# Layer 0's destination rows by one-hot matmul behind an earlier branch, and layer 1's node rows made inside layer 0's MLP loop

## The chip, the cores and the metric

One core of a Trainium2 chip runs the whole kernel in one launch. A core has five engines that each take their own instructions in order: PE (TensorE, matmuls; its weight loads, PEld, are shown apart), DVE (VectorE), ACT (ScalarE), POOL (GpSimd, which here issues the gathers) and SP (SyncE, which issues the plain DMAs). They meet through semaphores. The metric is the device time of one execution in microseconds (us); lower is better. The number for a kernel is the median of several runs.

## The reference

A graph network of four layers, each a graph step (`gnn`) and a per-node network (`ffn`), each on a layernorm of x and added to it. x has 3125 rows (nodes) of 256; there are 53125 edges sorted by destination, 50000 of them random and one loop per node. The change touches the two steps of layer 0 and the beginning of layer 1's graph step:

```python
def _L0_gnn_ref(...):
    xt = jnp.matmul(x, weight).reshape(-1, heads, out_ch)          # 4 heads of 64
    row, col = (edge_index[0], edge_index[1])
    alpha_l = jnp.einsum('ehd,hd->eh', xt[row], attn_l)
    alpha_r = jnp.einsum('ehd,hd->eh', xt[col], attn_r)
    alpha = jax.nn.softmax(jax.nn.leaky_relu(alpha_l + alpha_r, 0.01), axis=1)
    tmp = jnp.einsum('nh,nhd->nd', alpha[:n], xt[col[:n]])         # the first 3125 edges only
    out = jnp.broadcast_to(tmp[:, None, :], (n, heads, out_ch))

def _L0_ffn_ref(...):
    weights = (jnp.einsum('bsd,do->bso', x, wr) + br)[..., 0]      # one score per row
    _, idx = jax.lax.top_k(weights, k)                             # the better half, less one
    h = jax.nn.gelu(jnp.einsum('bkd,dh->bkh', sel, w1) + b1)       # 256 -> 1024
    y = jnp.einsum('bkh,hd->bkd', h, w2) + b2                      # 1024 -> 256
    y = y * w_sel[..., None]
    return processed + x                                           # rows not chosen: x

def _L1_gnn_ref(...):
    q = (x @ Wq + bq).reshape(n, H, C)
    k = (x @ Wk + bk).reshape(n, H, C)
    v = (x @ Wv + bv).reshape(n, H, C)
    e = (edge_attr @ We).reshape(-1, H, C)
    ...                                                            # attention over the edges
    out = out + x @ Ws + bs
```

Only the first 3125 edges count in layer 0's graph step, since `alpha` is cut to n rows.

## The kernel before

x stays on the chip as 25 tiles of 128 rows (`self.x`, 3200 rows with padding). The edges are 416 tiles of 128; 8 edge tiles (`EL`) make a window. As the edges are sorted by destination, the destinations of a window lie within 128 successive rows that begin at `W0[g]`, a constant. A flag worked out on the device (`prepare_flags`) says whether the input is so ordered; `sorted_edges()` reads it, and a branch takes the path that uses windows (`l1_gnn_sorted`, `after_l1_gnn_sorted`) or a general one.

The order of the instructions on each engine is fixed when the kernel is built, by a scheduler that goes by the dependences and by the buffers of the pools: a tile that is asked for again under the same name gets one of `bufs` buffers, and waits until its last reader is done.

What runs, in order:

- `l0_gnn` (L1407). Layernorm of x, and per tile of 128 rows a product with the weight and the two attention vectors; 264 columns go to the DRAM table `xt_d`, and the four columns of `alpha_l` once more to `al_d`. SP issues these 50 writes. `prepare_loads` loads what the flag and the indices need. Then five chunks of five edge tiles: for each tile POOL gathers `z` (4 values a row, by source) and `g` (264 values, by destination), both at L258; DVE and ACT do the softmax over the four heads and the weighted sum (L1435 to L1450), and the last line adds it to x.
- `l0_ffn` (L1452). Zero fills of tables that later layers need; layernorm of x, added to x (L234), transposed to `xT`; the row score `wa` for all rows; its copy by column, `wt` (L1487). Then the MLP over seven groups (`GROUPS`: six of four tiles, one of one): for each of eight hidden blocks a product of 128x512 into `ph` (two buffers) and a gelu on ACT (L1497), then for each tile eight matmuls and a bias matmul into `po`, copied by ACT to `yo` (L1504). Beside it DVE counts for each row how many rows have a better score (L1513 to L1517), sums this to `rank` (L1521), and makes `cw` (L1523): the score where the row is among the chosen, else 0. `prepare_flags` follows. The last loop (L1526) does x += yo * cw per tile.
- the branch.
- `l1_gnn_sorted` (L501). Four weights and four biases are loaded; layernorm of x, transposed to `xT`; `project` makes 512 columns per tile with a bias matmul of three bf16 rows (`ones3`), in three `pkv` buffers: first all 25 tiles of k and v, copied by ACT (L537) and written to `kv_d`; then all 25 tiles of q and the skip term, q split into three bf16 parts by ACT and DVE (`split`, L441 to L445) and written to `q_d`, the skip term added to x (L544). Then the edge loop: edge attributes `ea` times `We`, gathers of k and v by source, and q of the destination by a one-hot product (`window`, L453 and L456, gives the one-hot `sT`).

`split` writes an f32 tile as three bf16 tiles whose sum is the tile: two operations on ACT, two on DVE. `window(load, g)` loads the window's local destinations, broadcast to 128 partitions (256 KB), and compares them with the partition's number.

Of the kernel before, what the change touches and what calls it, by code (L numbers as in the profile page):

```python
# [8 lines left out]
F32 = mybir.dt.float32  # L9
BF = mybir.dt.bfloat16  # L10
I32 = mybir.dt.int32
AF = mybir.ActivationFunctionType
ALU = mybir.AluOpType
AX = mybir.AxisListType
PSUM = bass.MemoryType.PSUM
DRAM = bass.MemoryType.DRAM

P = 128
D = 256
N = 3125  # L20
NT = 25
NP = NT * P
# [4 lines left out]
EL = 8  # L27
# [4 lines left out]
GROUPS = [(g, min(4, NT - g)) for g in range(0, NT, 4)]  # L32
# [3 lines left out]
W0 = [min(max(round(N * (g + 0.5) * EL * P / E) - P // 2, 0), NP - P) for g in range(NW)]  # L36
# [10 lines left out]
class Net:  # L47
# [445 lines left out]
    def accumulate(self, work, table, acc, g):  # L493
# [4 lines left out]
        nc.scalar.copy(o, acc)  # L498
        nc.gpsimd.dma_start(table[W0[g]:W0[g] + P, :], o, accum_op=ALU.add)

    def l1_gnn_sorted(self, wp):  # L501
        nc, tc = self.nc, self.tc
        scale = 1.0 / 32 ** 0.5
        wkv = wp.tile([P, 2, 2, D], F32, name="wkv")
        for j, n in enumerate("kv"):
            nc.sync.dma_start(wkv[:, :, j, :],
                              self.ins[f"L1_gnn_W{n}"].rearrange("(k p) n -> p k n", p=P))
        wqs = wp.tile([P, 2, 2, D], F32, name="wqs")
        for j, n in enumerate("qs"):
            nc.sync.dma_start(wqs[:, :, j, :],  # L510
                              self.ins[f"L1_gnn_W{n}"].rearrange("(k p) n -> p k n", p=P))
        bkv = self.bias3(wp, "L1_gnn_bk", "L1_gnn_bv")
        bqs = self.bias3(wp, "L1_gnn_bq", "L1_gnn_bs")
        we = self.rows(wp, "L1_gnn_We")
        with ExitStack() as ctx:
            dram = ctx.enter_context(tc.tile_pool(name="d1", bufs=1, space=DRAM))
            kv_d = dram.tile([NP, 2 * D], F32, name="kv_d")
            q_d = dram.tile([NP, 3, D], BF, name="q_d")
            acc_d = self.acc1_d
            with ExitStack() as ctx1:  # L520
                big = ctx1.enter_context(tc.tile_pool(name="big", bufs=1))
                work = ctx1.enter_context(tc.tile_pool(name="work", bufs=3))
                psum = ctx1.enter_context(tc.tile_pool(name="psum", bufs=2, space=PSUM))
                xT = big.tile([P, 2, NP], F32, name="xT")
                self.layernorm(work, psum, xT=xT)

                def project(t, w, b):
                    p = psum.tile([P, 2, D], F32, name="pkv", bufs=3)
                    self.mm(p.rearrange("p j n -> p (j n)"),
                            [(xT[:, k, t * P:(t + 1) * P], w[:, k].rearrange("p j n -> p (j n)"))  # L530
                             for k in range(2)] + [(self.ones3, b)])
                    return p

                for t in range(NT):
                    p = project(t, wkv, bkv)
                    kv = work.tile([P, 2, D], F32, name="kv", bufs=6)
                    nc.scalar.copy(kv, p)  # L537
                    nc.sync.dma_start(kv_d[t * P:(t + 1) * P, :], kv.rearrange("p j n -> p (j n)"))
                for t in range(NT):
                    p = project(t, wqs, bqs)  # L540
                    q = work.tile([P, 3, D], BF, name="q")
                    self.split(work, q, p[:, 0, :], D, "q")
                    nc.sync.dma_start(q_d[t * P:(t + 1) * P, :, :], q)
                    nc.vector.tensor_add(self.x[:, t, :], self.x[:, t, :], p[:, 1, :])  # L544
            big = ctx.enter_context(tc.tile_pool(name="big", bufs=1))
            load = ctx.enter_context(tc.tile_pool(name="load", bufs=2))
            work = ctx.enter_context(tc.tile_pool(name="work", bufs=3))
            psum = ctx.enter_context(tc.tile_pool(name="psum", bufs=2, space=PSUM))
# [7 lines left out]
            for c in range(ET // 2 + LAG):  # L556
                if c < ET // 2:
                    t = 2 * c
                    if t % EL == 0:
                        g = t // EL  # L560
                        ea = load.tile([P, 2, EL * P], F32, name="ea")
                        nc.sync.dma_start(ea, self.ins["edge_attr_256"][:, :, t * P:(t + EL) * P])
                        sT = self.window(load, g)
                        qw = load.tile([P, 3, D], BF, name="qw")
                        nc.sync.dma_start(qw, q_d[W0[g]:W0[g] + P, :, :])
                    kv = work.tile([P, 2, 2 * D + 8], F32, name="kv", bufs=LAG + 5)
# [3 lines left out]
                    for j in range(2):  # L570
                        self.gather(kv[:, j, :2 * D], kv_d, self.idx["src"][:, t + j:t + j + 1])
                        e = slice((t + j) % EL * P, ((t + j) % EL + 1) * P)
# [20 lines left out]
                b = c - LAG  # L593
                if b >= 0:
                    kv = kvs.pop(b)
                    t = 2 * b
# [810 lines left out]
    def l0_gnn(self, wp):  # L1407
        nc, tc = self.nc, self.tc
        w = self.with_attention(wp, "L0_gnn_weight", 4, ("L0_gnn_attn_l", "L0_gnn_attn_r"))
        with ExitStack() as ctx:  # L1410
            dram = ctx.enter_context(tc.tile_pool(name="d0", bufs=1, space=DRAM))
            big = ctx.enter_context(tc.tile_pool(name="big", bufs=1))
            work = ctx.enter_context(tc.tile_pool(name="work", bufs=3))
            psum = ctx.enter_context(tc.tile_pool(name="psum", bufs=2, space=PSUM))
            xt_d = dram.tile([NP, D + 8], F32, name="xt_d")
            al_d = dram.tile([NP, 4], F32, name="al_d")
            xT = big.tile([P, 2, NP], F32, name="xT")
            self.layernorm(work, psum, xT=xT)
            for t in range(NT):
                pt = psum.tile([P, D + 8], F32, name="pt")  # L1420
                self.mm(pt, [(xT[:, k, t * P:(t + 1) * P], w[:, k, :]) for k in range(2)])
                row = work.tile([P, D + 8], F32, name="row", bufs=6)
                nc.scalar.copy(row, pt)
                nc.sync.dma_start(xt_d[t * P:(t + 1) * P, :], row)
                nc.sync.dma_start(al_d[t * P:(t + 1) * P, :], row[:, D:D + 4])
            self.prepare_loads()

            C = 5
            for t0 in range(0, NT, C):
                z = work.tile([P, C, 4], F32, name="z")  # L1430
                g = work.tile([P, C, D + 8], F32, name="g")
                for j in range(C):
                    self.gather(z[:, j, :], al_d, self.idx["src"][:, t0 + j:t0 + j + 1])
                    self.gather(g[:, j, :], xt_d, self.idx["dst"][:, t0 + j:t0 + j + 1])
                nc.vector.tensor_add(z, z, g[:, :, D + 4:])  # L1435
                nc.vector.scalar_tensor_tensor(z, z, 0.01, z, op0=ALU.mult, op1=ALU.max)
                mx = work.tile([P, C], F32, name="mx")
                mb = mx.unsqueeze(2).to_broadcast([P, C, 4])
                nc.vector.tensor_reduce(mx, z, axis=AX.X, op=ALU.max)
                nc.vector.tensor_sub(z, z, mb)  # L1440
                nc.scalar.activation(z, z, AF.Exp)
                nc.vector.tensor_reduce(mx, z, axis=AX.X, op=ALU.add)
                nc.vector.reciprocal(mx, mx)
                nc.vector.tensor_mul(z, z, mb)
                gv = g[:, :, :D].rearrange("p t (h d) -> p t h d", h=4)
                nc.vector.tensor_mul(gv, gv, z.unsqueeze(3).to_broadcast([P, C, 4, 64]))
                nc.vector.tensor_add(gv[:, :, :2], gv[:, :, :2], gv[:, :, 2:])
                nc.vector.tensor_add(gv[:, :, 0, :], gv[:, :, 0, :], gv[:, :, 1, :])
                xv = self.x[:, t0:t0 + C, :].rearrange("p t (h d) -> p t h d", h=4)
                nc.vector.tensor_add(xv, xv, gv[:, :, :1, :].to_broadcast([P, C, 4, 64]))  # L1450

    def l0_ffn(self, wp):  # L1452

        nc, tc = self.nc, self.tc
        keep = int(0.5 * N) - 1
# [6 lines left out]
        with ExitStack() as ctx:  # L1462
# [58 lines left out]
            nc.vector.tensor_reduce(rank, cnt, axis=AX.X, op=ALU.add)  # L1521
            cw = big.tile([P, NT], F32, name="cw")
            nc.vector.scalar_tensor_tensor(cw, rank, float(keep), wt, op0=ALU.is_lt, op1=ALU.mult)  # L1523
            self.prepare_flags()
            for t in range(NT):
                nc.vector.scalar_tensor_tensor(self.x[:, t, :], yo[:, t, :], cw[:, t:t + 1],  # L1526
                                               self.x[:, t, :], op0=ALU.mult, op1=ALU.add)


    def l1_gnn(self, wp):  # L1530
# [684 lines left out]
@with_exitstack  # L2215
def tile_gnn_ffn(ctx: ExitStack, tc: tile.TileContext, ins, out):
    net = Net(ctx, tc, ins, out)

    def run(*layers):
        for layer in layers:  # L2220
            with tc.tile_pool(name="w", bufs=1) as wp:
                layer(wp)

    run(net.l0_gnn, net.l0_ffn)

    with tc.If(net.sorted_edges()) as cmp:
        run(net.l1_gnn_sorted, net.after_l1_gnn_sorted)
    with cmp.Else():
        run(net.l1_gnn, net.l1_ffn, net.l2_gnn, net.l2_ffn, net.l3_gnn, net.l3_ffn)


# [72 lines left out]
```

## Time and profile before

| what | us |
|---|---|
| median of 5 runs (lowest, highest) | 3863.33 (3857.88, 3866.10) |
| profiled execution | 3859.73 |
| its span in the profile | 3857.9 |
| first gather of layer 0 starts, last ends | 68.74, 136.38 |
| x complete after layer 0's edges | 150.9 |
| first MLP matmul of layer 0 | 179.66 |
| `cw` is made | 278.4 |
| last combine of layer 0 (L1526) | 363.4 |
| first matmul after the branch | 375.69 |
| last projection matmul of layer 1 ends | 495.4 |
| first add of the edge loop (L576) starts | 510.61 |

Times of single instructions are counted from the span's start. PE is busy 85% of the span, DVE 58%, POOL 43%, ACT 25%, and the mean granted clock of PE is 0.917. All that the change touches lies in the first 510 us; the rest is layer 1's edges and its network, and layers 2 and 3.

In the rows below, a group is named by line, engine, operation, output <- inputs, shape, type and count; behind the bar stand its busy time in us and the mean ns of one, then the idle time of its engine before it and what ended that. In a table by stage each engine has its busy time and, in brackets, the number of instructions.

### The profile page before, as it was taken

How to read it: one execution, taken by the hardware profiler on the slowest of the kernel's cores; microseconds unless marked ns; L12 is line 12 of the kernel's file. 1: busy time of each engine (PE TensorE's matmuls, PEld its weight loads, DVE VectorE, ACT ScalarE, POOL GpSimd, SP SyncE). 2: the span in 40 equal slices, each digit the busy share in tenths (PEclk: the TensorE clock that was granted, in tenths of full speed). 3: DMA queues.
4: the chain of work that ended last, by engine and by line, in shares of the span. 5: the costliest groups of instructions: out<-in, count | busy, mean ns of one | idle time of the engine just before them, and what ended most of it. 6: DMA issues, size and time to landing. Idle time of an engine off the chain costs nothing. (4 is left out here: it accounts for less than half of the span.)

```text
span 3857.9 us, 46616 instructions
## 1 busy us (share of the span) xinstructions
PE 3283.2 (85%) x15463; PEld 2293.4 (59%) x15463; DVE 2219.1 (58%) x5521; ACT 965.6 (25%) x2102; POOL 1673.5 (43%) x1510
## 2 busy tenths in 40 slices
PE   3498989999999356799999998799999936867789
PEld 2265367777777144577777776456666625655654
DVE  4692279999999624643443343433333347877762
ACT  2222300000000212444444443333333301101132
POOL 3300056666665122777777777000000077777300
PEclk7699999999999677899999999899999958888889
DMA  4550278888887166887777776300000065555200
GB/s 135 167 183 17 101 270 275 277 274 284 272 273 208 48 209 187 197 151 132 132 131 130 130 132 92 102 0 6 6 6 6 19 192 148 146 149 146 63 12 23
DMA packets 340139, 524.10 MB, mean 136 GB/s; under 512 B 64495, under 2 KB 247089, under 8 KB 339889
## 3 DMA queue, kind: packets, MB, share of 16 engines
q0 software_dynamic: 125040, 236.91, 28.6%
q1 hardware_dynamic: 207457, 276.76, 22.8%
q10 hardware_dynamic: 7392, 7.34, 0.6%
q8 instruction: 126, 2.06, 0.2%
q14 instruction: 124, 1.02, 0.1%
HBM read 389.15 MB, written 131.64 MB: 135 GB/s over the span
## 5 line engine op out<-in xcount | busy, mean ns | idle before, releaser
L1137 POOL DMA_INDIRECT t<-sm,to x416 | 660.0, 1586 | 197.0 <-ACT sm L1134 86.1
L258 POOL DMA_INDIRECT kv<-kv_d,src_i x416 | 415.2, 998 | 606.5 <-DVE s L462 348.5
L258 POOL DMA_INDIRECT xa<-xa_d,src_i x416 | 400.1, 962 | 131.0 <-issue 110.6
L205 PE MATMUL pe<-L_gnn_We,ea 128*128 128x256 f32 x1664 | 438.7, 386 | 12.3 <-DMA ea<-in_edge_attr_dram 9.6
L1120 PE MATMUL pf<-L_gnn_Wf,hf 128*128 128x256 f32 x1664 | 421.1, 396 | 7.1 <-ACT hf L1083 7.1
L800 PE MATMUL acc<-xa,s 128*128 128x272 f32 x1312 | 345.2, 420 | 78.6 <-DVE s L791 77.4
L205 PEld LDWEIGHTS <-sT 128*128 128x128 bf16 x3152 | 267.9, 99 | 164.0 <-issue 52.7
L1123 DVE TENSOR_TENSOR xs<-xs,pf 128x512 f32<-128x512 f32 x208 | 142.9, 687 | 376.4 <-PE pf L1120 376.2
L1120 PEld LDWEIGHTS pf<-L_gnn_Wf,hf 128*128 128x128 f32 x1664 | 303.6, 192 | 88.6 <-issue 47.0
L800 PEld LDWEIGHTS acc<-xa,s 128*128 128x128 f32 x1312 | 261.4, 205 | 138.2 <-DVE s L791 80.9
L205 PEld LDWEIGHTS pe<-L_gnn_We,ea 128*128 128x128 f32 x1664 | 292.3, 192 | 67.3 <-DVE kv L576 26.9
L145 POOL MEMSET sel<- 4x256 f32 x1 | 0.3, 302 | 673.4 <-PE tp L205 673.4
L576 DVE TENSOR_TENSOR kv<-kv,pe 128x1024 f32<-128x1024 f32 x208 | 251.4, 1209 | 4.0 <-PE pe L205 4.0
L604 PE MATMUL acc<-kv,s 128*128 128x264 f32 x832 | 226.9, 398 | 11.0 <-DVE kv L599 8.7
L1292 ACT ACTIVATE h<-ph,L_ffn_b,bn_r 128x512 f32<-128x512 f32 (+1 forms) x224 | 162.7, 731 | 290.7 <-PE ph L205 290.3
L1134 ACT COPY sm<-ps 128x512 f32<-128x512 f32 x208 | 121.9, 586 | 451.2 <-PE ps L1132 377.9
L1320 DVE SCALAR_TENSOR_TENSOR xres<-po,v,xres 128x256 f32<-128x256 f32 x200 | 96.2, 482 | 238.4 <-PE po L205 238.2
L1132 PE MATMUL ps<-xs,m 128*128 128x256 f32 x832 | 217.1, 384 | 18.5 <-DVE xs L1123 13.7
L205 PE MATMUL qx<-qw,sT 128*128 128x256 bf16 x1248 | 189.5, 274 | 3.2 <-DVE al L579 1.3
L205 PE MATMUL po<-L_ffn_Wo,h 128*128 128x256 f32 x800 | 191.8, 383 | 0.0
L205 PE MATMUL ph<-xT,L_ffn_W 128*128 128x512 f32 (+1 forms) x448 | 186.6, 554 | 1.0 <-ACT h L1292 1.0
L1132 PEld LDWEIGHTS ps<-xs,m 128*128 128x128 f32 x832 | 159.4, 192 | 42.2 <-issue 7.6
(440 smaller groups left out, 5372.0 us busy)
## 6 DMA issues: line engine op xcount, KB each, us to landing
ea<-in_edge_attr_dram SPq DMA_DIRECT2D x52, 1024.0 KB
dl<-dlT_d SPq DMA_DIRECT2D x156, 256.0 KB
row<-src_d SPq DMA_DIRECT2D x52, 512.0 KB
xs_d<-zero SPq DMA_DIRECT2D x2, 7168.0 KB
xg<-xs_d SPq DMA_DIRECT2D x28, 512.0 KB
t<-zero SPq DMA_DIRECT2D x4, 3328.0 KB
seg<-seg_d SPq DMA_DIRECT2D x52, 256.0 KB
qw<-q_d SPq DMA_DIRECT2D x52, 192.0 KB
```

Source lines behind the costliest of these rows:

```text
L205: self.nc.tensor.matmul(out, l, r, start=(i == 0), stop=(i == len(pairs) - 1))
L258: self.nc.gpsimd.indirect_dma_start(out=out, out_offset=None, in_=table, in_offset=bass.IndirectOffsetOnAxis(ap=ids, axis=0))
L576: nc.vector.tensor_add(kvv, kvv, pe[:, :, None, :].to_broadcast([P, 2, 2, D]))
L604: nc.tensor.matmul(acc, s1[:, j, :], kv[:, j, D:], start=((t + j) % EL == 0), stop=((t + j) % EL == EL - 1))
L800: nc.tensor.matmul(accs[T][:, :R + 8], s1[:, i, :], xa[:, j, :], start=begins and i == 0, stop=last[T] == b and j == js[-1])
L1120: nc.tensor.matmul(pf[:, j, :], hf[:, c % 4, k, j * P:(j + 1) * P], wf2[:, k, :], start=False, stop=j + k == 2)
L1123: nc.vector.tensor_mul(xs, xs, pf)
L1132: nc.tensor.matmul(ps[:, j, :], m[:, (2 * c + j) % EL, :], xs[:, j, :], start=True, stop=True)
L1134: nc.scalar.copy(sm, ps)
L1137: nc.gpsimd.indirect_dma_start(out=tables[(2 * c + j) % len(tables)], in_=sm[:, j, :], in_offset=None, compute_op=ALU.add, out_offset=bass ...
L1292: nc.scalar.activation(h[:, f, :w], ph[:, :w], AF.Relu, scale=ab[i][0][:, c:c + 1], bias=ab[i][1][:, c:c + 1])
L1320: nc.vector.scalar_tensor_tensor(xv[:, i, :], po[:, i, :], v[:, j + i, e - 2:e - 1], xv[:, i, :], op0=ALU.mult, op1=ALU.add)
```

## The change

The branch goes from behind `l0_ffn` to behind the dense part of `l0_gnn`. To that end `prepare_flags` moves up to the front of `l0_gnn`, right behind `prepare_loads`, and the edge part of `l0_gnn` becomes a function of its own, `l0_edges`. The general path calls it as it was. The sorted path calls `until_l1`, which loads layer 1's weights, runs `l0_edges(by_dst=True)` and then `l0_ffn` with a function to be called after each group's combine.

With `by_dst`, the rows of `xt_d` by destination aren't gathered: four windows of 128 rows are loaded whole and split into three bf16 parts, and each edge tile takes three one-hot matmuls and a copy by ACT.

The function called after each group, `l1_rows`, does for the group's tiles what `l1_gnn_sorted` did in front of its edge loop: layernorm, transposes into the MLP's own `xT`, both projections (now in the two `ph` buffers of the MLP's pool), the q split, the writes, the skip term. The bias of k and v is no longer a matmul but a DVE add with a bias tile spread over the partitions; `kv` has two buffers instead of six. `We` is still loaded at the start of `l1_gnn_sorted`.

```diff
+    def l1_weights(self, wp):
...
+        b = wp.tile([P, 2, D], F32, name="bkv")
+        for j, n in enumerate("kv"):
+            a = self.ins[f"L1_gnn_b{n}"]
+            nc.sync.dma_start(b[:, j, :], bass.AP(tensor=a.tensor, offset=a.offset,
+                                                  ap=[[0, P], [1, D]]))
+        return *ws, b, self.bias3(wp, "L1_gnn_bq", "L1_gnn_bs")
+    def l1_rows(self, weights, work, psum, xT, t0, n):
+        nc = self.nc
+        wkv, wqs, bkv, bqs = weights
+        y = work.tile([P, 5, D], F32, name="ln_y", bufs=2)
+        self.normalised(work, y, t0, n)
+        for j in range(n):
+            self.transposed(psum, xT, y[:, j, :], t0 + j)
+        for t in range(t0, t0 + n):
+            def project(w):
+                p = psum.tile([P, 2, D], F32, name="ph")
+                return p, p.rearrange("p j n -> p (j n)"), [
+                    (xT[:, k, t * P:(t + 1) * P], w[:, k].rearrange("p j n -> p (j n)"))
+                    for k in range(2)]
+            p, o, pairs = project(wkv)
+            self.mm(o, pairs)
+            kv = work.tile([P, 2, D], F32, name="kv")
+            nc.vector.tensor_add(kv, p, bkv)
+            nc.sync.dma_start(self.kv_d[t * P:(t + 1) * P, :], kv.rearrange("p j n -> p (j n)"))
+            p, o, pairs = project(wqs)
+            self.mm(o, pairs + [(self.ones3, bqs)])
+            q = work.tile([P, 3, D], BF, name="q")
+            self.split(work, q, p[:, 0, :], D, "q")
+            nc.sync.dma_start(self.q_d[t * P:(t + 1) * P, :, :], q)
+            nc.vector.tensor_add(self.x[:, t, :], self.x[:, t, :], p[:, 1, :])
+    def until_l1(self, wp):
+        self.kv_d = self.dram.tile([NP, 2 * D], F32, name="kv_d")
+        self.q_d = self.dram.tile([NP, 3, D], BF, name="q_d")
+        weights = self.l1_weights(wp)
+        self.l0_edges(wp, by_dst=True)
+        self.l0_ffn(wp, lambda *a: self.l1_rows(weights, *a))
...
     def l0_gnn(self, wp):
...
+            self.prepare_loads()
+            self.prepare_flags()
             xT = big.tile([P, 2, NP], F32, name="xT")
             self.layernorm(work, psum, xT=xT)
...
-            self.prepare_loads()
+    def l0_edges(self, wp, by_dst=False):
...
+            if by_dst:
+                for g in range((NT + EL - 1) // EL):
+                    xw = load.tile([P, D + 8], F32, name="xw")
+                    nc.sync.dma_start(xw, xt_d[W0[g]:W0[g] + P, :])
+                    x3 = load.tile([P, 3, D + 8], BF, name="x3")
+                    self.split(work, x3, xw, D + 8, "x")
+                    wins.append((x3, self.window(load, g)))
...
-                    self.gather(z[:, j, :], al_d, self.idx["src"][:, t0 + j:t0 + j + 1])
-                    self.gather(g[:, j, :], xt_d, self.idx["dst"][:, t0 + j:t0 + j + 1])
+                    t = t0 + j
+                    self.gather(z[:, j, :], al_d, self.idx["src"][:, t:t + 1])
+                    if by_dst:
+                        x3, sT = wins[t // EL]
+                        e = slice(t % EL * P, (t % EL + 1) * P)
+                        p = psum.tile([P, D + 8], F32, name="pg")
+                        self.mm(p, [(sT[:, e], x3[:, i, :]) for i in range(3)])
+                        nc.scalar.copy(g[:, j, :], p)
+                    else:
+                        self.gather(g[:, j, :], xt_d, self.idx["dst"][:, t:t + 1])
...
-            self.prepare_flags()
-            for t in range(NT):
-                nc.vector.scalar_tensor_tensor(self.x[:, t, :], yo[:, t, :], cw[:, t:t + 1],
-                                               self.x[:, t, :], op0=ALU.mult, op1=ALU.add)
+            for t0, n in GROUPS:
+                for t in range(t0, t0 + n):
+                    nc.vector.scalar_tensor_tensor(self.x[:, t, :], yo[:, t, :], cw[:, t:t + 1],
+                                                   self.x[:, t, :], op0=ALU.mult, op1=ALU.add)
+                if then is not None:
+                    then(work, psum, xT, t0, n)
...
-    run(net.l0_gnn, net.l0_ffn)
+    run(net.l0_gnn)
     with tc.If(net.sorted_edges()) as cmp:
-        run(net.l1_gnn_sorted, net.after_l1_gnn_sorted)
+        run(net.until_l1, net.l1_gnn_sorted, net.after_l1_gnn_sorted)
     with cmp.Else():
-        run(net.l1_gnn, net.l1_ffn, net.l2_gnn, net.l2_ffn, net.l3_gnn, net.l3_ffn)
+        run(net.l0_edges, net.l0_ffn, net.l1_gnn, net.l1_ffn, net.l2_gnn, net.l2_ffn, net.l3_gnn, net.l3_ffn)
```

More of the change, by code (lines that the diff above doesn't have):

```diff
@@ L499, in accumulate @@
         nc.gpsimd.dma_start(table[W0[g]:W0[g] + P, :], o, accum_op=ALU.add)
+    def l1_weights(self, wp):
+        nc = self.nc
+        ws = []
+        for names in ("kv", "qs"):
+            w = wp.tile([P, 2, 2, D], F32, name=f"w{names}")
+            for j, n in enumerate(names):
+                nc.sync.dma_start(w[:, :, j, :],
+                                  self.ins[f"L1_gnn_W{n}"].rearrange("(k p) n -> p k n", p=P))
+            ws.append(w)
+        b = wp.tile([P, 2, D], F32, name="bkv")
[5 more added lines that the diff above has]
+    def l1_rows(self, weights, work, psum, xT, t0, n):
+        nc = self.nc
+        wkv, wqs, bkv, bqs = weights
[26 more added lines that the diff above has]
+        self.l0_ffn(wp, lambda *a: self.l1_rows(weights, *a))
     def l1_gnn_sorted(self, wp):
@@ L503, in l1_gnn_sorted @@
         scale = 1.0 / 32 ** 0.5
[L504 to L512, printed above, removed]
@@ L513, in l1_gnn_sorted @@
-        bqs = self.bias3(wp, "L1_gnn_bq", "L1_gnn_bs")
         we = self.rows(wp, "L1_gnn_We")
+        kv_d, q_d, acc_d = self.kv_d, self.q_d, self.acc1_d
         with ExitStack() as ctx:
[L516 to L532, printed above, removed]
-                for t in range(NT):
[L535 to L544, printed above, removed]
@@ L1410, in l0_gnn @@
         with ExitStack() as ctx:
-            dram = ctx.enter_context(tc.tile_pool(name="d0", bufs=1, space=DRAM))
             big = ctx.enter_context(tc.tile_pool(name="big", bufs=1))
@@ L1414, in l0_gnn @@
             psum = ctx.enter_context(tc.tile_pool(name="psum", bufs=2, space=PSUM))
-            xt_d = dram.tile([NP, D + 8], F32, name="xt_d")
-            al_d = dram.tile([NP, 4], F32, name="al_d")
+            self.xt_d = xt_d = self.dram.tile([NP, D + 8], F32, name="xt_d")
+            self.al_d = al_d = self.dram.tile([NP, 4], F32, name="al_d")
+            self.prepare_loads()
+            self.prepare_flags()
             xT = big.tile([P, 2, NP], F32, name="xT")
@@ L1425, in l0_gnn @@
                 nc.sync.dma_start(al_d[t * P:(t + 1) * P, :], row[:, D:D + 4])
-            self.prepare_loads()
+    def l0_edges(self, wp, by_dst=False):
+        nc, tc = self.nc, self.tc
+        xt_d, al_d = self.xt_d, self.al_d
+        with ExitStack() as ctx:
+            load = ctx.enter_context(tc.tile_pool(name="load", bufs=4))
+            work = ctx.enter_context(tc.tile_pool(name="work", bufs=3))
+            psum = ctx.enter_context(tc.tile_pool(name="psum", bufs=6, space=PSUM))
+            wins = []
+            if by_dst:
[5 more added lines that the diff above has]
+                    wins.append((x3, self.window(load, g)))
             C = 5
@@ L1450, in l0_gnn, with l0_ffn @@
                 nc.vector.tensor_add(xv, xv, gv[:, :, :1, :].to_broadcast([P, C, 4, 64]))
-    def l0_ffn(self, wp):
+    def l0_ffn(self, wp, then=None):
         nc, tc = self.nc, self.tc
@@ L1523, in l0_ffn @@
             nc.vector.scalar_tensor_tensor(cw, rank, float(keep), wt, op0=ALU.is_lt, op1=ALU.mult)
-            self.prepare_flags()
-            for t in range(NT):
-                nc.vector.scalar_tensor_tensor(self.x[:, t, :], yo[:, t, :], cw[:, t:t + 1],
-                                               self.x[:, t, :], op0=ALU.mult, op1=ALU.add)
+            for t0, n in GROUPS:
[4 more added lines that the diff above has]
+                    then(work, psum, xT, t0, n)
     def l1_gnn(self, wp):
```

## The prediction

> **What bounds the kernel now.** The change touches the first 510 us only, so I read the page's slices first (each 96.4 us), then the busy time by stage, then the single rows in which one stage hands over to the next. The slices of PE, DVE and POOL:
>
> ```profile
> PE   3498989999999356799999998799999936867789
> DVE  4692279999999624643443343433333347877762
> POOL 3300056666665122777777777000000077777300
> ```
>
> PE is part idle in the first slices. By stage (start:end, length, then busy us and instruction count of PE, weight load, DVE, ACT, POOL, granted clock, DMA share, GB/s):
>
> ```profile
> 64.00:140.00 76.00, 0.60 (x2) 0.29 (x2) 21.60 (x71) 4.93 (x8) 52.70 (x50) 0.52 0.30 90
> 140.00:180.00 40.00, 25.41 (x102) 14.15 (x102) 32.27 (x102) 15.20 (x39) 0.32 (x1) 0.72 0.73 240
> 180.00:238.00 58.00, 58.00 (x200) 36.20 (x198) 56.99 (x86) 14.44 (x24) 0.00 (x0) 1.00 1.04 346
> 238.00:287.00 49.00, 49.00 (x161) 29.15 (x160) 45.83 (x79) 13.23 (x22) 0.00 (x0) 1.00 0.13 43
> 287.00:364.00 77.00, 75.84 (x293) 50.72 (x291) 5.81 (x12) 18.41 (x36) 0.00 (x0) 1.00 0.00 0
> 364.00:376.00 12.00, 0.32 (x2) 0.34 (x3) 11.43 (x50) 1.70 (x3) 0.00 (x0) 0.64 0.34 111
> 376.00:497.00 121.00, 119.39 (x300) 44.86 (x298) 43.32 (x143) 42.26 (x103) 0.00 (x0) 0.98 0.25 94
> ```
>
> 64 to 140 is layer 0's edge stage, set by POOL's 50 gathers. From 180 to 364 PE does the MLP without a gap. 364 to 376 is a hole in which layer 1's layernorm waits for the MLP's end. 376 to 497 is PE again: layer 1's projections. One thing beside it matters: DVE is full from 180 on with layer 0's rank counts, and they end here:
>
> ```profile
> 278.13 0.26 DVE L1521 TENSOR_REDUCE rank<-cnt 128x25 f32<-128x100 f32 x1
> 278.43 0.19 DVE L1523 SCALAR_TENSOR_TENSOR cw<-rank,wt 128x25 f32<-128x25 f32 x1
> 278.72 4.84 DVE L1526 SCALAR_TENSOR_TENSOR xres<-yo,cw,xres 128x256 f32<-128x256 f32 x12
> ```
>
> `cw` is the per-row factor by which every MLP row enters x. Before 278.6 no row of x is final, though the MLP has finished three of its seven groups.
>
> **Part 1: half of the gathers go.** The rows of the two kinds:
>
> ```profile
> L258 POOL DMA_INDIRECT g<-xt_d,dst_i x25 | 27.2, 1090 | 44.4 <-DMA xt_d<-row 37.0 <-issue 7.3
> L258 POOL DMA_INDIRECT z<-al_d,src_i x25 | 25.5, 1018 | 7.6 <-issue 7.3 <-DMA z<-al_d,src_i 0.3
> ```
>
> The 50 start at 68.74 and the last ends at 136.38: 67.6 us. The 25 that stay cost 1.02 + 0.29 idle each, 32.3 us with the pitch's few long ones (bounds 31.5 and 43.8, by the shortest usual pitch of 1.26 and the longest, 1.75). In their place come four windows (a row load, a 256 KB broadcast and its one-hot compare at 0.56, a split of two ACT and two DVE operations at 0.4) and 75 bf16 matmuls. A 128x264 one is not in the trace; the warm 128x256 one (`qx<-qw,sT`) took 274 ns, and at the clock of 0.52 in this stage twice that bounds it: 21 to 41 us over a stage in which PE did 0.6. I take 41: it still lies beside the gathers. The copies, 25 at 0.4 on ACT (busy 4.9 of 76), lie there too. Without that cover the matmuls would cost up to 9 us.
>
> When do the gathers start? The flag chain now stands ahead of the normalising of tiles 10 to 14 on DVE, and the branch ahead of them on POOL. But SP issues 50 row writes at about 0.97 us each until 65.5, and that set the first gather before; I keep 68.5 (66.5 to 70). Behind the branch SP first issues eight weight and bias loads (0.24 to 0.47 each, 3.2 us) ahead of the first window; the window is wanted by the first matmuls only, and these have 30 us of slack.
>
> The last gather then ends at 100.8, its data are on DVE 1.9 later (136.38 to 138.28 before). In the built order the chunk that needs them stands ahead of the heavy part of chunks 2 to 4: three times 1.48 + 0.81 + 0.49 + 1.48 = 4.26, 12.8, plus 2.1 of small ones. x is complete at 117.6, against 150.9. From there to the MLP's first matmul (179.66) it was 28.8; the first layernorm chunk, earlier done under the gathers, now adds 23.8 / 4 = 5.9. The MLP starts at 152.2: **-27.5** (-22 to -32).
>
> **Part 2: layer 1's rows inside the MLP's loop.** Here the order of PE's instructions decides, and in the changed program it stands so: groups 0 and 1 as before; in the third group three of eight first-layer products (5.2 us) and two second-layer matmuls (0.9), and then the transpose of layer 1's first normalised tile. PE takes its instructions in order. That transpose needs `ln_y`, this needs x, x needs `cw`. ACT has the same: its square root for that tile stands before the second gelu of the group. In the clock of before, PE is there at 238.4 + 6.1 = 244.5. `cw` is done at 278.6, four combines (1.6), four statistics, four more combines that stand between, the root and the scaling follow: 286.7. So PE stands still for **42.2 us** in a stage where it was full. Rank counts start with the MLP's start, so this doesn't depend on part 1.
>
> After it, in before's clock:
> - the rest of the MLP: 362.9 - 244.4 = 118.5
> - ten tiles' transposes among it, 0.53 each: 5.3
> - PE's clock after the wait, and ACT table loads that end late: 3. Before, the clock was 0.50 from 375 to 381, after 12.8 us of idleness, 6 us at half speed
> - the last group of one tile is too short to cover two table loads at 1.28: 2.6
> - all projections stand behind the MLP, as they share the `ph` buffers with it: per tile 1.73 for kv (the pitch of `ph`) and 2.23 for q and s, 99.0, and 15 transposes, 8.0
> - 1.5 for the handover
>
> 286.7 + 118.5 + 5.3 + 3 + 2.6 + 107 + 1.5 = 524.6, where the last projection ended at 495.4 before: **+29.2**. In it are two gains: the hole of 12.8 us is gone, and the bias matmul of kv:
>
> ```profile
> L537 ACT COPY kv<-pkv 128x512 f32<-128x512 f32 x25 | 14.7, 589 | 32.0 <-PE pkv L205 32.0
> L205 PE MATMUL pkv<-L_gnn_bk,ones 3*128 3x512 bf16 x25 | 9.6, 384 | 0.0
> L445 DVE TENSOR_TENSOR q<-q_r,q 128x256 bf16<-128x256 f32 x25 | 10.6, 425 | 3.6
> ```
>
> (25 at 0.384 and the 0.12 around each, 12.5.) The bias is added on DVE instead, from PSUM, 0.59 (the ACT copy) to 0.69 (the nearest DVE row, 128x512 at L1123); I take 0.69. DVE's work per tile is then 1.93, beside PE's 3.96. It must free a `ph` buffer before PE comes round to it two products later: kv's is free 0.75 after its product, the next product on it starts 2.23 after. Covered. SP's two writes a tile move along with the projections; nothing else waits in its queue there but `We` and the first edge attributes.
>
> Two rules of the Trainium skill bear on this; the sum above doesn't use them. "ScalarE: Activation LUTs", What ACT_TABLE_LOAD costs, has 2.66 us for every switch, a load of 1283 ns and a drain of 1380, and advises to do all of one set before switching; this change puts roots among gelus. The trace has the load at 1283 ns, and a root at 368.87 right behind the load at 367.58, so I see no drain; by the page fourteen switches would be an estimated 37 us of ACT, and by the row 18, under a PE that is busy. "TensorE: Matmul & The Clock Gate", Part 1, has the clock fall after an idle window of some 3.4 us; the rows at 375 agree and show a recovery of 6, and by the page's 3.4 the term of 3 would be nearer 2.
>
> **Part 3: the lead-in of layer 1's edges.** Edge attributes and the first broadcast were issued behind the q writes (499.3 and 500.0, product at 505.1, first add at 510.6). Now the loads stand ahead of the last q write, and `We` before them: -2.5 (-5 to +3).
>
> Sum: -27.5 + 29.2 - 2.5 = -0.8 against 3859.73. The median of the five runs is 3.6 above that execution, so 3862.5; I say 3863.
>
> **The rivals.**
> A, the wait does not bind: if the root and the transpose of layer 1's rows came after the MLP's groups on PE and ACT, the 42.2 us would go and the time be 3863 - 42 = 3821. For it: DVE is nearly free after 287 (5.8 of 77 busy), so layer 1's rows could be prepared there. Against it: the order of the instructions on PE and ACT, which is fixed.
> B, slower: the projections are held by their two `ph` buffers. Before, `pkv` had three and six kv buffers and ACT copied. If each kv add runs only after DVE's queue of the previous tile's q work (0.42 + 0.41 + 0.42) and PE waits for it, 0.75 a tile, 25 times: +19, 3882. It decides from 0.3 us a tile. For it: three DVE operations per tile now stand round each add. Against: DVE at 1.93 of 3.96.
> C, part 1 gives less: the flag chain delays the rows, or POOL's pitch stays long. At 1.5 per gather it is +6, 3869.
> That the branch isn't taken is excluded: the lines of the sorted path (L462, L576, L604) ran.
>
> **How the numbers follow.** A measurement of this kernel can tell 0.2%, 7.7 us, from no change. The main case has 0.55 (0.05 faster, 0.43 within, 0.07 slower), A 0.15, B 0.20, C 0.08 (0.03 within), no effect 0.02. Faster 0.20, same 0.48, slower 0.32. The main case by its bounds: down 4.5 (start), 2.5 (lead-in), 4 (clock and tables at nothing); up 5.5, 5.5, 2.5: 3852 to 3876. The range takes in B with a margin: 3850 to 3885; A lies outside.
>
> **What would show it.** PE idle for about 42 us right before the first `tp<-ln_y` of the MLP loop, released by DVE, at 217 to 259 in the new clock: the main step; less than 20 speaks for A. The first MLP matmul near 152. Per-tile pitch of the projections 3.96; 4.3 or more, with DVE's kv add as the releaser, is B. Gathers' end near 101; 110 is C. First kv add of the edges near 510. I'd be wrong if rows behind 510 moved too: nothing there is changed.

## The result, and the profile after

| | before | after |
|---|---|---|
| median (lowest to highest), us | 3861.85 (3853.49 to 3869.80), 46 runs | 3862.86 (3855.42 to 3868.18), 25 runs |
| span of the profiled execution | 3857.9 | 3864.6 |
| first gather of layer 0 starts | 68.7 | 71.4 |
| first MLP matmul of layer 0 | 179.7 | 155.0 |
| `cw` is made | 278.4 | 253.8 |
| last projection matmul of layer 1 ends | 495.4 | 490.9 |
| first add of the edge loop | 510.6 | 509.8 |
| last `acc` matmul of layer 1's edges starts | 1257.9 | 1250.7 |

The ratio of after to before is 1.0003, 95% interval [0.9997, 1.0008]: no difference. The forecast was 3863.

The slices of PE, DVE and POOL, each 96.6 us:

```profile
PE   4659989999998356799999999799999927876889
DVE  5872479999999534644334333433333347777762
POOL 3100056666664112777777777000000077777300
```

The stages of the changed kernel, cut at its own hand-overs (columns as in the table by stage of before):

```profile
64.00:112.00 48.00, 13.65 (x78) 9.12 (x77) 21.45 (x61) 13.12 (x40) 29.54 (x25) 0.65 0.43 120
112.00:155.00 43.00, 23.09 (x103) 12.73 (x103) 38.70 (x129) 15.08 (x40) 0.32 (x1) 0.75 0.72 238
155.00:220.00 65.00, 64.98 (x219) 39.54 (x217) 63.72 (x95) 17.12 (x27) 0.00 (x0) 1.00 1.00 331
220.00:262.00 42.00, 0.04 (x1) 0.07 (x2) 41.69 (x91) 2.75 (x4) 0.00 (x0) 0.53 0.00 0
262.00:387.00 125.00, 123.75 (x454) 79.79 (x454) 27.31 (x92) 45.14 (x78) 0.00 (x0) 0.98 0.00 1
387.00:491.00 104.00, 102.74 (x256) 41.01 (x255) 50.22 (x115) 24.82 (x66) 0.00 (x0) 1.00 0.29 108
```

POOL has half of its gathers left, and in the place of the others stand matmuls (groups; busy us and mean ns behind the bar):

```profile
L258 POOL DMA_INDIRECT z<-al_d,src_i x25 | 29.5, 1182 | 44.7 <-issue 43.1 <-DVE mx L1477 1.6
L205 PE MATMUL pg<-x,sT 128*128 128x264 bf16 x75 | 13.0, 344 | 23.0 <-DMA dl<-dlT_d 15.5 <-ACT g L1470 7.6
```

The MLP starts 24.7 us earlier. Then, in the table, there is a new row, 220 to 262: PE does nothing (0.04 us), DVE is full, and no transfer runs. The old hole at 364 is gone: from 262 to 491 PE is idle for 2.5 us in all. This is what stands around the new one on PE and on DVE (two timelines; start, duration, and in brackets the idle time before):

```profile
218.95 1.03 PE L205 MATMUL po<-L_ffn_w,ht 128*128 128x256 f32 x4
261.96 1.08 PE L253 MATMUL tp<-ident,ln_y 128*128 128x128 f32 x4 [41.98 <-DVE ln_y L246]
```

```profile
253.76 0.19 DVE L1562 SCALAR_TENSOR_TENSOR cw<-rank,wt 128x25 f32<-128x25 f32 x1
254.06 1.67 DVE L1565 SCALAR_TENSOR_TENSOR xres<-yo,cw,xres 128x256 f32<-128x256 f32 x4
...
261.40 1.38 DVE L246 TENSOR_SCALAR ln_y<-xres,ln_mv,ln_r 128x256 f32<-128x256 f32 x4
```

PE stops in the third group, waits 41.98 us for `ln_y`, and that comes 7.6 us after `cw`. The gelus stop too: ACT had loaded the table for the root at 216.48 and stood 40.83 us in front of it:

```profile
216.48 1.28 ACT L214 ACT_TABLE_LOAD   x1
258.60 0.20 ACT L214 ACTIVATE ln_r<-ln_v 128x4 f32<-128x4 f32 x1 [40.83 <-DVE ln_v L212]
258.82 1.28 ACT L1536 ACT_TABLE_LOAD   x1
260.11 1.26 ACT L1536 ACTIVATE ht<-ph,L_ffn_b 128x512 f32<-128x512 f32 x2
```

### The profile page after: what moved, and what is told of

The parts are those of the page before. It is cut to its first block, busy times and chain, and to the rows that moved or that the text cites. A ratio compares the mean times of both kernels' runs of the same rounds, so it can differ in the third digit from the quotient of the medians.

```text
span 3864.6 us, 46767 instructions
## 1 busy us (share of the span) xinstructions
PE 3289.7 (85%) x15513; PEld 2302.0 (60%) x15513; DVE 2246.2 (58%) x5565; ACT 974.5 (25%) x2122; POOL 1645.6 (43%) x1485
## 3 DMA queue, kind: packets, MB, share of 16 engines
q8 instruction: 126, 2.06, 0.2%
## 5 line engine op out<-in xcount | busy, mean ns | idle before, releaser
L205 PEld LDWEIGHTS <-sT 128*128 128x128 bf16 x3227 | 276.5, 99 | 190.6 <-issue 77.8
L1147 ACT COPY sm<-ps 128x512 f32<-128x512 f32 x208 | 121.9, 586 | 455.8 <-PE ps L1145 381.1
L205 PE MATMUL xe<-xw,sT 128*128 128x256 bf16 x1248 | 173.3, 276 | 16.0 <-DMA xw<-x_d 9.5
```

Source lines behind the costliest of these rows:

```text
L205: self.nc.tensor.matmul(out, l, r, start=(i == 0), stop=(i == len(pairs) - 1))
L1147: nc.scalar.copy(sm, ps)
```

## The experiments

The kernels ran in four groups, each on a chip of its own, with the kernel before beside them; its median was 3859.97 on the first chip, 4115.39 on the second, 4109.63 on the third and 3852.36 on the last. On the second and third, layer 3's edges take 690 to 700 us from the first `acc` matmul to the last, where they take 505 on the others, and layer 1's edge loop (from its first add to its last `acc` matmul) takes 767 to 771 instead of 741 to 747. So ratios are compared, and stretches within the first 1500 us; those that hold the edge loop are compared only within one chip, or between the first and the last.

**One part alone.** In the first of the two, `l1_gnn_sorted` is the old one and `until_l1` is cut down:

```diff
     def until_l1(self, wp):
 
-        self.kv_d = self.dram.tile([NP, 2 * D], F32, name="kv_d")
-        self.q_d = self.dram.tile([NP, 3, D], BF, name="q_d")
-        weights = self.l1_weights(wp)
         self.l0_edges(wp, by_dst=True)
-        self.l0_ffn(wp, lambda *a: self.l1_rows(weights, *a))
+        self.l0_ffn(wp)
...
```

> The early branch and the one-hot rows alone; layer 1's rows are made behind layer 0's MLP as before. Theory W (the gain of part 1 is real and is given back by the wait for cw inside the MLP): the MLP starts at 155 as in the changed kernel, 24.7 us earlier than before, and everything behind keeps that: first add of the edge loop near 486, time 3837. Theory L (what is gained ahead of layer 1's edge loop is lost again behind it, in layer 1's expert network): first add near 486 as well, but the time falls by 16 or less, 3846 or more.

Measured: 3839.64 against 3859.97, ratio 0.9947 [0.9934, 0.9961]. The MLP starts at 154.1, the first add of the edge loop is at 485.0 and the loop ends 26.9 us earlier than before in the profiled execution; the medians differ by 20.3. That lies between 3837 and 3846, nearer to theory W, but a part of L may be in it.

In the second, the rows of layer 1 stay in the loop and the gathers are all kept (the branch stays in its new place):

```diff
-        self.l0_edges(wp, by_dst=True)
+        self.l0_edges(wp)
```

> Layer 1's rows inside the MLP's loop, with all 50 gathers of layer 0 kept. Theory W: PE stands still for 42 us in the third group, and from the MLP's first matmul to the edge loop's first add it takes the 354.8 us of the changed kernel against 331.0 before, so 3862 + 24 = 3886. Theory L: slower by 16 or less, 3878 or below.

Measured: 3887.07, ratio 1.0077 [1.0062, 1.0092]. PE's longest wait from 150 us on (a row of the table of waits: total, times, longest):

```profile
PE tp L253 <- DVE ln_y L246: 42.6, 2, 42.0
```

From the MLP's first matmul to the first add it took 354.6 us, in the changed kernel 354.8, in the kernel before 330.9, with part 1 alone 330.9. With part 2 alone the MLP started at 182.8, in the kernel before at 179.7, so some of the loss may lie ahead of the MLP. One part gives 20 us and the other takes 27 away, each known to about 5 or 6; by these intervals their sum, +7, can't be told from the +1.0 of both together.

**The wait moved.** `cw` is made to depend on a late row of the MLP's result, so that the layer-1 rows come later in the order of PE and ACT:

```diff
             nc.vector.tensor_reduce(rank, cnt, axis=AX.X, op=ALU.add)
+            late = big.tile([P, 1], F32, name="late")
+            nc.vector.tensor_scalar(late, yo[:, NT - 1, 0:1], 0.0, None, op0=ALU.mult)
+            nc.vector.tensor_scalar(rank, rank, late, None, op0=ALU.add)
             cw = big.tile([P, NT], F32, name="cw")
```

> The changed kernel with cw made to depend on the last yo, so that layer 1's rows begin when the MLP is done. Theory W: no wait of PE inside the MLP, a hole of about 8 us and a cold clock behind it; the last projection ends near 463 against 490.9, and the time is 3863 - 28 = 3835. Theory P (not the wait costs, but that the projections stand behind the MLP in two ph buffers, evicted by DVE): the rows are no nearer to the MLP, and the time stays within 8 us of 3863.

Measured: 3834.40, ratio 0.9933 [0.9913, 0.9954]. The six runs lie in two clumps, 3824.5 to 3827.2 and 3841.6 to 3845.4, and the median falls between them; why is not known, and the profiled one is of the upper (3842.17). PE's waits in the stretch:

```profile
PE tp L253 <- DVE ln_y L246: 10.1, 1, 10.1
PE tp L253 <- ACT xT L254: 1.5, 6, 0.2
```

42 us have become 10.1, and the last projection ends at 460.4 (the first begins at 353.2). The projections are behind the MLP as before, in the same two buffers: theory P falls, by either clump.

With `yo[:, 15, 0:1]` in place of `yo[:, NT - 1, 0:1]`:

> The same with cw made to depend on yo of tile 15, the last of the fourth group; PE's first transpose of layer 1 then stands in the sixth group, some 50 us after the rank counts are done. Theory W: no wait and no hole; the last projection ends near 453, the time is 3863 - 38 = 3825, faster than both kernels. Theory P: within 8 us of 3863.

Measured: 3821.67, ratio 0.9900 [0.9885, 0.9915], faster than both kernels. PE's waits from the MLP's start to the last projection:

```profile
PE tp L253 <- ACT xT L254: 1.7, 6, 0.5
PE ph L205 <- ACT xT L254: 0.5, 1, 0.5
PE pw L1525 <- ACT wa L1520: 0.3, 1, 0.3
```

No wait above 0.5 us is left. The first transposes of layer 1 stand inside the sixth group (306.60), and the MLP runs into the projections without a gap (341.06):

```profile
306.60 0.60 PE L253 MATMUL tp<-ident,ln_y 128*128 128x128 f32 x4
...
340.68 0.55 PE L253 MATMUL tp<-ident,ln_y 128*128 128x128 f32 x3
341.06 1.88 PE L205 MATMUL ph<-wkv,xT 128*128 128x512 f32 x4
```

From the MLP's start to the first add: 309.6, against 354.8 in the changed kernel and 330.9 before. So the layer-1 rows in the MLP's loop are worth 21 us by this stretch, and 18 by the medians of this kernel and of part 1 alone, once the order doesn't put them ahead of their own input.

**Where some of the gain goes.** On the first chip every kernel is slower behind the edge loop than the kernel before is there. The stretch of layer 1's expert network (from its first transpose `tp<-ident,xg` to the first `ph<-rb` matmul of layer 2), whose code isn't touched, took 121.9 us before, and 131.4, 131.2, 126.5, 135.5 and 130.9 in the changed kernel and its four variants.

> The kernel before, profiled once more, for the stage of layer 1's expert network (from its first transpose of gathered rows to the first matmul of layer 2's edges): it took 121.9 us in the kernel before and 126.5 to 135.5 in the changed kernel and its four variants. Theory L (the changed kernels really are slower there): about 122 again. Theory S (this stage scatters from execution to execution, whatever the kernel): anything between 120 and 136, above 126 as likely as not.

> The same a second time. Theory L: about 122. Theory S: 120 to 136.

> The changed kernel, profiled once more, for the same stage, which took 131.4. Theory L: 128 to 136. Theory S: 120 to 136. In both, PE's wait in the MLP is 42 us again, and the edge loop of layer 1 ends near 1251.

Measured: 122.9 and 120.8 for the kernel before, 127.3 for the changed one (whole 4122.42, 4108.36 and 4132.03, one execution each). The kernel before doesn't scatter there by more than 2.1 us, as theory L has it; the changed kernel is slower again, but scatters by 4, and 127.3 is just below the 128 that L gave as its least. PE's wait in the MLP was 42.0 again. The loop's end near 1251 wasn't met: the MLP started at 159.4, and the loop ended at 1283.2, 6 us later than in the two profiles of the kernel before beside it instead of 7 earlier; the profiled executions of the changed kernel differ by 4 us already at the MLP's start.

Does the place of the DRAM tables do it? The change takes `xt_d`, `al_d`, `kv_d` and `q_d` from the long-lived pool; here only that is done to the kernel before:

```diff
-            dram = ctx.enter_context(tc.tile_pool(name="d1", bufs=1, space=DRAM))
-            kv_d = dram.tile([NP, 2 * D], F32, name="kv_d")
-            q_d = dram.tile([NP, 3, D], BF, name="q_d")
+            kv_d = self.dram.tile([NP, 2 * D], F32, name="kv_d")
+            q_d = self.dram.tile([NP, 3, D], BF, name="q_d")
...
-            dram = ctx.enter_context(tc.tile_pool(name="d0", bufs=1, space=DRAM))
...
-            xt_d = dram.tile([NP, D + 8], F32, name="xt_d")
-            al_d = dram.tile([NP, 4], F32, name="al_d")
+            xt_d = self.dram.tile([NP, D + 8], F32, name="xt_d")
+            al_d = self.dram.tile([NP, 4], F32, name="al_d")
```

> The kernel before with its four DRAM tables xt_d, al_d, kv_d, q_d taken from the long-lived pool, as in the changed kernel, and nothing else. The stage of layer 1's expert network took 120.8 to 122.9 us in three profiles of the kernel before, 127.3 and 131.4 in two of the changed kernel, 126.5 to 135.5 in its variants, with the same order of instructions on PE and SP. Theory D (where the tables lie in DRAM slows the loads of that stage): 127 or more here too, and the whole about 8 us slower than before. Rival: 121 to 123 and no difference to before; then the place of the tables is not the cause.

Measured: 124.0 us in the stretch, ratio 1.0003 [0.9991, 1.0016]. Theory D falls.

The rows of the stretch say where the time lies, first before, then in the changed kernel (columns as in the table by stage):

```profile
1380.90:1502.80 121.90, 87.49 (x450) 68.70 (x450) 44.86 (x73) 26.09 (x56) 12.69 (x27) 0.84 0.76 223
1377.50:1508.90 131.40, 97.14 (x450) 74.47 (x450) 44.88 (x74) 26.20 (x56) 13.13 (x27) 0.73 0.70 206
```

The same 450 instructions keep PE busy for 97.1 us instead of 87.5, at a granted clock of 0.73 instead of 0.84; in this pair that is all of the 9.5 us. The four profiles with the old front part have 0.83 to 0.86 and 85 to 88 us, the ten others 0.73 to 0.81 and 90 to 97, and in some of these PE is idle for longer too. Why the clock is lower there, with nothing changed in the stretch, stays open.

**The last write of q.** In the changed kernel SP issues the edge attributes ahead of it, and DVE's first one-hot `s` waits for it:

```profile
491.40 0.68 SPq L575 DMA_DIRECT2D ea<-in_edge_attr_dram  x1
492.77 0.33 SPq L541 DMA_DIRECT2D q_d<-q  x1
```

```profile
499.34 1.10 DVE L462 TENSOR_TENSOR s<-iota,dloc 128x256 f32<-128x256 f32 x3 [6.61 <-DMA q_d<-q]
```

In the kernel before, `s` waited 1.99 us. POOL's first gather stands behind `s` (500.16, and 500.05 before, although the projections end 4.5 us earlier). The kernel with the rows from the sixth group, with the write first:

```diff
+        self.last_q = c.tile([P, 1], F32, name="last_q")
...
             nc.vector.tensor_add(self.x[:, t, :], self.x[:, t, :], p[:, 1, :])
+            if t == NT - 1:
+                nc.vector.tensor_copy(self.last_q, q[:, 2, :1])
...
+                        if g < 2:
+                            nc.vector.tensor_copy(ea[:, 0, :1], self.last_q)
                         nc.sync.dma_start(ea, self.ins["edge_attr_256"][:, :, t * P:(t + EL) * P])
```

> The kernel with layer 1's rows from the sixth group, and the first two loads of edge attributes issued behind the last write of q instead of ahead of it. Theory Q (DVE's first one-hot and POOL's first gather of the edge loop wait 6.3 us for that write, which stands behind 1 MB of edge attributes in the DMA queue): the write lands 2 to 3 us after its issue as before, the gathers start 4 us earlier, and the time falls by 3 to 4, to 3818. Rival (the loop is bound by DVE and by the edge attributes, which now come later): no change within 2, 3822.

Measured: ratio 0.9927 [0.9902, 0.9951], 4087.60, on a chip where the kernel before took 4115.39, so that it can't be set against 3821.67; `s` waits 0.7 us for that write and the stretch up to the first add is 306.3. Both once more on one chip:

> The kernel with layer 1's rows from the sixth group once more, as the measure for the next one on the same chip: a ratio to before of 0.990 as in the first run.

> The kernel with the last write of q ahead of the edge attributes, on the same chip as the one it is made from. From the MLP's first matmul to the first add of the edge loop it took 306.3 us against 309.6. Theory Q: 3 us faster than that kernel in the whole. Rival (DVE binds the edge loop, and takes back what the first gathers win): the same time within 2 us.

Measured: 4080.23 (ratio 0.9924 [0.9906, 0.9942]) without, 4081.49 (0.9927 [0.9909, 0.9945]) with the write first. The stretch to the first add is 309.3 and 306.2, so the 3 us are there, and the loop behind it is 769.5 and 767.5, so it takes nothing back; the whole doesn't show it. The time fits the rival, but each ratio is known to 7 us only, which leaves room for theory Q's 3. The reason that the rival gave (DVE in the loop) isn't borne out.

**The next layer's constants.** Every kernel with the rows in the MLP took 126.6 to 129.3 us from the end of the edge loop to the expert network, the others 123.0 to 125.0. What differs is when SP issues the constants of the next layer, in the kernel before and in the changed one:

```profile
1237.21 0.82 SPq L129 DMA_DIRECT2D L_gnn_bu<-in_L_gnn_bu_dram  x2
```

```profile
1271.01 0.83 SPq L129 DMA_DIRECT2D L_gnn_bu<-in_L_gnn_bu_dram  x2
```

The last kernel, with the rows from the sixth group, keeps the room of the weights that have left the pool:

```diff
     def l1_gnn_sorted(self, wp):
...
+        for n in ("kv", "qs"):
+            keep = wp.tile([P, 2, 2, D], F32, name=f"keep{n}")
+            nc.vector.memset(keep[:1, 0, 0, :1], 0.0)
         we = self.rows(wp, "L1_gnn_We")
```

> The kernel with layer 1's rows from the sixth group, with two tiles of the old size of layer 1's weights kept in the weight pool of the edge loop. Every kernel that makes layer 1's rows inside the MLP issued the next layer's constants 20 us behind the end of layer 1's edge loop (1271.0 against 1250.7) instead of 20 us ahead of it (1237.2 against 1257.9), and took 126.6 to 129.3 us from that end to the first transpose of the expert network, where the kernels with the weights in the old place took 123.0 to 125.0. Theory M (the weights have left the pool, the next layer's constants now fall on buffers of the edge loop and wait for them): the constants are issued ahead of the loop's end again, and this stretch takes 123 to 125; the time is 4 us less than that kernel's (ratio to before 0.989 instead of 0.990 or 0.991 instead of 0.992, less than the interval can tell). The expert network's own stretch behind it stays at 126 or more if it has another cause, and falls to 121 to 124 if it has this one. Rival (the constants are not waited for): 126.6 or more as before.

Measured: 3816.61 against 3852.36, ratio 0.9901 [0.9883, 0.9919]. The constants go out at 1200.5, 10.6 us ahead of the loop's end, and the stretch takes 123.8, where the same kernel without the room had 127.0: theory M is right about the cause. The 4 us that it gave for the whole can't be seen: 0.9901 against 0.9900. The loop itself takes 743.9 instead of 742.1, so that of 3.2 us 1.8 seem to be paid inside it. In the same way the kernel before has 747.3 + 123.0 and the changed one 740.9 + 126.8; but on the second and third chip the loop takes 769.1 to 770.5 with early constants and 767.5 to 769.7 with late ones, so this isn't shown. The expert network's stretch stays at 129.6: it has another cause.

## Why the prediction was right, point by point

- **Part 1, -27.5: measured -24.7.** The gathers began at 71.4 instead of 68.5; SP's row writes lasted until 68.0 (66.0 before). 25 of them took 38.2 us instead of 32.3 (mean 1182 ns, one of 3.22 us, and one wait of 1.6 us for DVE to free a `z` buffer). Why single gathers took longer isn't shown. The bound of 43.8 rested on 1.75 as the longest pitch; that was the duration of one gather, and one of 2.06 stood in the rows of before. x was complete at 124.1 instead of 117.6. From there to the MLP 30.9 instead of 34.6. The matmuls that stood in for the gathers were hidden, as forecast, and cheaper than both bounds (21 and 41): 344 ns each, which makes 25.8, but 13.0 us of PE in all, as they overlap.
- **Rival C, part 1 gives less: its sign came.** The gathers ended at 109.6, where 110 was named for C, and in the nine profiles with part 1 at 107.5 to 114.3. Its price came too, 5.9 us in the gathers for the 6 named; 2.3 between the last gather and x, and 3.7 from x to the MLP, were won back. Part 1 is also smaller than this pair has it: the MLP starts at 177.0 to 179.7 in the four profiles with the old front part and at 153.3 to 160.1 in the nine with part 1, 20.9 apart on average, which fits the 20.3 of part 1 alone.
- **The wait, 42.2: measured 41.98**, at the place forecast. PE was there 65.0 us after the MLP's start (64.8 forecast).
- **Behind it, terms of 129.4 for the rest of the MLP: measured 125.0.** The transposes, the cold clock, the tables and the small last group were put at 10.9 together and took 6.5. The clock was 0.50 to about 266, 4 us; the ten table loads of 1.28 us behind the wait cost PE one wait of 1.14.
- **Projections, 108.5 with the handover: measured 104.0**, 3.95 us a tile (3.96 forecast), and 5.3 for the transposes instead of 8.0. Rival B had its answer here: the row of kv's add shows 0.69 us each, and PE waited for no `ph` buffer.

```profile
L535 DVE TENSOR_TENSOR kv<-ph,bkv 128x512 f32<-128x512 f32 x25 | 17.3, 692 | 6.9 <-PE ph L205 4.6
L205 PE MATMUL ph<-wqs,xT 128*128 128x512 f32 x100 | 47.0, 592 | 0.0
```

- **Part 2 in all, +29.2: measured +20.2** (335.9 from the MLP's start to the last projection, 315.8 before): too dear by 9.0.
- **The lead-in, -2.5: wrong in its direction.** From the last projection to the first add it took 18.8 us, before 15.2. The step took it that loading edge attributes ahead of the last q write is a gain; the write came behind them and `s` waited.
- **Up to the first add: -0.8 measured, -0.8 forecast, and that is luck.** Part 2 was too dear by 9.0, against a part 1 that fell short by 2.8 and a lead-in that was off by 6.1. Each step stands by itself, and the sum met the time because these three cancel.
- **What the sum left out.** It had nothing behind the first add, and gave as a sign of being wrong that rows behind 510 move too, since nothing there is changed. They moved: the next layer's constants went out 34 us later, the edge loop with the stretch behind it was 2.6 us shorter, the expert network 9.5 longer in this pair, and 4 to 14 longer than its 121.9 in the variants with part 1. In this pair of profiles the spans differ by 6.7 us, while the medians differ by 1.0: the profiled execution was 3.4 above its median after the change, and 2.1 below it before. So how much of the loss behind the first add is in the medians isn't known.

Rival A was wrong as stated, since the wait does bind in the changed kernel, and nearly right as a price: with the rows three groups later the ratio is 0.9900 instead of 1.0003, some 40 us, where it said 42. Theory W's 3825 and the measured 3821.67 agree with it.

## What to carry to other kernels

When work of a later stage is put into the loop of an earlier one, look where it stands in each engine's fixed order, and when its input is ready at that place: here PE and ACT stood 42 us in front of a result that DVE needed 99 us to make, and moving the same work three groups on turned no change into 1% less. A part that gains and a part that loses can hide each other to 0.03%; each alone showed it at once. And a buffer that leaves a pool can change which later loads may start early: the next layer's constants went out 20.4 us behind the loop's end, and 10.6 ahead of it once its room was kept.

## What the runs showed of the hardware

- A DMA that writes 192 KB, issued 1.4 us behind loads of 1 MB and more, was waited for until 6.6 us after its issue (492.77 to 499.34); issued ahead of them (the second kernel with the write first), until 3.5 us after its issue (452.97 to 456.48).
- Matmuls of 32-bit operands after 42 us of idleness ran at a granted clock of 0.50 for some 4 us, then 0.87 and 1.00 (stretches of 2 us from 262 on). "TensorE: Matmul & The Clock Gate", Part 1, has the clock come back after about 3.4 us of work; 4 is near that.
- A table load of 1.28 us was followed by the next activation at once or within 0.25 us (load 263.47, root 264.76; load 264.99, gelu 266.50), in the ten switches of the MLP that stand behind the wait; the drain of 1380 ns that "ScalarE: Activation LUTs", What ACT_TABLE_LOAD costs, adds to each switch is not seen in these rows.
- The expert network's stretch is 7 us longer, 129.4 against 122.4 on average of two profiles of the changed kernel and four of kernels with the old front part, with the same order of instructions on PE and SP, at a granted clock of 0.73 and 0.78 against 0.83 to 0.86. Why is open.
